# Issue order of gathers and weight additions, smaller paced copies, and three small moves in a transformer-block kernel

## The chip, the cores and the metric

The kernel runs on one core of a Trainium2 chip. A core has a matrix engine (TensorE, "PE" in profiles), a vector engine (VectorE, "DVE"), an engine for activations and copies (ScalarE, "ACT"), a general engine (GpSimd, "POOL") and an engine that mostly issues transfers (SyncE, "SP"). Each engine executes its own instructions in order; they meet through semaphores. The metric is the device time of one execution in microseconds, and of several runs the median.

## The reference

Input is `x` of 8 batches with 256 tokens of 512 features. Two layers follow one another, each a mixer and a mixture of experts with a residual:

```python
x = x + ffn0(attention(x))
x = x + ffn1(lora_linear(x))
```

The attention has 8 query heads and 4 key/value heads of 64. Keys and values are normalised, rotated and written into a paged cache (blocks of 16 rows) at a position that each batch gives; a token sees 256 positions back:

```python
k_blocks = k_blocks.at[blk, :, off, :].set(k)      # v likewise
k_all = k_blocks[block_tables]                     # (B, G, S, HD)
scores = where(allowed, q @ k_all.T * SCALE, -inf)
o = softmax(scores) @ v_all;  return o @ Wo.T
```

The experts of layer 0 share a base weight, and each of 8 experts adds a sparse difference to it. There are 4096 entries; entry `s` lands at row `mask_idx[s] // H` and column `mask_idx[s] % H`:

```python
deltas   = softmax(expert_atom_weights) @ atoms            # (8, 4096)
weighted = deltas * sigmoid(importance)
vals     = sum_k rw[t, k] * weighted[top_idx[t, k]]        # two experts for each token
contrib  = segment_sum((xt[:, cols] * vals).T, rows)       # added to xt @ W.T
```

Layer 1 is a linear map with one of 8 low-rank adapters for each batch, and then 8 experts with two matrices and a GELU, of which each token uses two, weighted by `alpha`.

## The kernel before

Four stages follow one another on TensorE.

*Projections*, up to about 99 us. `keys_values` (L1287) makes keys and values of 16 token tiles of 128 and stores them (`kv_new`). Beside this the 4096 sparse entries are prepared in 32 groups of 128: entries that hit the same place are added up (`sum_same`, L1410, result `sums`), and their places are found (`find_places`, L1435, result `put_i`). `spread_base` writes the base weight eight times into `delta_d`, a table in device memory with a row for each element of the matrix and a column for each expert.

*Attention*, about 122 to 409 us. The loop at L1684 goes over 8 batches. For batch `b` it issues the gathers of batch `b+2`: `gather_old` (L1178) reads 4 tiles of rows from the cache, `gather_new` (L1189) then overwrites the rows that this call has made. Both are indirect DMAs issued by GpSimd (L1193). Three sets of buffers `kv` go round by `b % 3`, so batch `b+2` takes the set that batch `b-1` gave up. Then come the queries of `b+2` (whose `roots`, L1244, GpSimd makes), `attend(b, 0)` for the first 128 tokens, `prepared(b+1)` (L1518: keys turned by TensorE into `pk`, copied to `KT`, and a mask), and `attend(b, 1)`. `attend` has four steps `m`: scores (`ps`, L1554), a masked maximum (VectorE), exponentials (ScalarE, L1585), transposes (`pp`), copies (`pT`, L1603), and the product with the values (`po`, L1608).

In each of the first batches six of the 32 groups of sums are added to `delta_d` (`add_delta`, L1262): an indirect DMA with addition, issued by GpSimd. Each waits until the one before has landed, because two groups may hit one row. A batch's six have `entries` as their source, a copy of the sums multiplied by `held`, which is 1 and is computed from the mask of batch `b+1`; so they can't be issued before `prepared(b+1)`.

In batches 6 and 7 half of the finished `delta_d` is loaded and rearranged for TensorE (`load_delta`, L730): eight tiles `raw` of 128x1024, each copied by ScalarE (L748). With `paced` each copy is kept in program order. `attend` takes a step of that work (`next(beside, None)`, L1620) after every second `m`.

*Experts of layer 0*, to about 584 us. Tokens are sorted by expert. `routing_constants` (L148) makes tables of small integers: GpSimd writes them by iotas and VectorE casts them. For layer 0 this is called at `b == 2` (L1706) with `late`, which keeps each VectorE operation in program order. One iota there, `count_i` (L181 and 182), shares the buffer of `low_i`. `fill_slots` (L303) makes lists of tokens by products with one-hot matrices (`pm`, L366); groups of four products are bound together by `in_a_row` (L112): the first is placed freely, the others directly behind it. The lists then steer fetches of token rows (`xs`), transposes (`pa`, copied to `xsT`, L698) and the products with the weights (`py`, L670 and L679).

*Folding, and layer 1*, from about 584 us. `fold_gate` (L1816) folds linear weights into the gate by `seen_through` (L121): products `pw`, copies `wn` (L130), products `acc` (L131). The copies are issued with `nc.any`, where the build chooses between VectorE and ScalarE. Beside this VectorE adds up `part` tiles that SyncE loads (L2020). Then come the linear map, its adapters, and the experts of layer 1, to about 952 us.

The order on each engine is settled at build time by a scheduler, which goes by dependencies and priorities. `tc.keep_in_program_order(x)` pins an instruction `x` behind the work that stands ahead of it in the text; unpinned ones may be moved.

Of the kernel before, what the change touches and what calls it, by code (L numbers as in the profile page):

```python
# [1 line left out]


# [16 lines left out]
P = 128  # L20
# [65 lines left out]
def two_layer_kernel(ctx: ExitStack, tc: tile.TileContext, io: dict, out: bass.AP):  # L86
# [24 lines left out]

    def in_a_row(products):  # L112

        for j, product in enumerate(products):
            if j == 0:
                product()
            else:
                with tc.high_priority():
                    tc.keep_in_program_order(product())
# [28 lines left out]
    def routing_constants(pool, plan=None, late=False, quads=False):  # L148

        after = tc.keep_in_program_order if late else lambda ins: ins
        earlier = pool.tile([P, P], F32, name="earlier")
# [11 lines left out]
        nc.gpsimd.iota(dif_i, pattern=[[1, NT * E]], base=0, channel_multiplier=-1)  # L165
        low_i = pool.tile([P, NT * E], I32, name="low_i")
        after(nc.vector.tensor_scalar(low_i, dif_i, E - 1, None, ALU.bitwise_and))
        dif = pool.tile([P, NT * E], F32, name="dif", tag="row")
        after(nc.vector.tensor_copy(dif, dif_i))
        ahead = pool.tile([P, NT * E], F32, name="ahead")  # L170
        after(nc.vector.tensor_copy(ahead, low_i))
        after(nc.vector.tensor_scalar(ahead, ahead, 0.0, None, ALU.is_equal))
        same_e = pool.tile([P, E], F32, name="same_e")
        after(nc.vector.tensor_copy(same_e, ahead[:, :E]))
        after(nc.vector.scalar_tensor_tensor(ahead, dif, 0.5, ahead, ALU.is_gt, ALU.mult))
        below_i = pool.tile([P, E, E], I32, name="below_i", tag="bl")
        nc.gpsimd.iota(below_i, pattern=[[1, E], [-1, E]], base=0, channel_multiplier=0)
        below_e = pool.tile([P, E, E], F32, name="below_e")
        after(nc.vector.tensor_copy(below_e, below_i))
        after(nc.vector.tensor_scalar(below_e, below_e, 0.5, None, ALU.is_gt))  # L180
        count_i = pool.tile([P, P], I32, name="count_i", tag="low_i")  # L181
        nc.gpsimd.iota(count_i, pattern=[[1, P]], base=0, channel_multiplier=0)
        count = pool.tile([P, P], F32, name="count")
        after(nc.vector.tensor_copy(count, count_i))
        tok_i = pool.tile([P, NT], I32, name="tok_i")
# [7 lines left out]
        else:  # L193
            nc.gpsimd.iota(tok_i, pattern=[[P, NT]], base=-N, channel_multiplier=1)
        tok = pool.tile([P, NT], F32, name="tok")
        after(nc.vector.tensor_copy(tok, tok_i))
        part_i = pool.tile([P, 1], I32, name="part_i")
        nc.gpsimd.iota(part_i, pattern=[[0, 1]], base=N, channel_multiplier=1)
        part = pool.tile([P, 1], F32, name="part")
        after(nc.vector.tensor_copy(part, part_i))  # L200
        fixed = None
        if plan:
            fixed_i = pool.tile([P, 6, E], I32, name="fixed_i")
            for j, values in enumerate(zip(*plan.by_expert)):
                e = 0
                while e < E:
                    step = values[e + 1] - values[e] if e + 1 < E else 0
                    end = e + 1
                    while end < E and values[end] == values[e] + step * (end - e):
                        end += 1  # L210
                    nc.gpsimd.iota(
                        fixed_i[:, j, e:end],
                        pattern=[[step, end - e]],
                        base=values[e],
                        channel_multiplier=0,
                    )
                    e = end
            fixed = pool.tile([P, 6, E], F32, name="fixed")
            after(nc.vector.tensor_copy(fixed, fixed_i))
        ones = pool.tile([P, 1], F32, name="ones")  # L220
        nc.gpsimd.memset(ones, 1.0)
        return earlier, ahead, same_e, below_e, count, tok, part, fixed, ones
# [80 lines left out]
    def fill_slots(keep, pool, psum, tag, consts, slot, rem, cf, n, at_once, quads, ways=1, hots=None):  # L303
# [18 lines left out]
        for j in range(0, 2 * nt, STEP):  # L322
# [32 lines left out]
            if ways == 1:  # L355
                for k in range(STEP):
                    nc.tensor.matmul(
                        pm,
                        hot[:, k, :],
                        put_all[:, (j + k) % at_once, :],  # L360
                        start=(j + k == 0),
                        stop=(j + k == 2 * nt - 1),
                    )
            else:
                in_a_row(
                    lambda k=k: nc.tensor.matmul(  # L366
                        pm[k % ways * wide : (k % ways + 1) * wide, :],
                        put_all[:, (j + k) % at_once, :],
                        hot[:, k, :],
                        start=(j == 0 and k >= STEP - ways),  # L370
                        stop=(j == 2 * nt - STEP and k < ways),
                    )
                    for k in reversed(range(STEP))
                )
        if ways > 1:
# [150 lines left out]
    def route_rest(keep, pool, psum, places, used_i):  # L526

        row, rows, left, coef, quads = places
        consts = routing_constants(pool, quads=quads)
        each = [P, NT, E]  # L530
# [198 lines left out]

    def load_delta(half, pool, engines, bufs, tag="raw", paced=False):  # L730

# [14 lines left out]
        for n, (k, cols) in enumerate(places):  # L746
            yield
            copy = engines[n % len(engines)](  # L748
                delta[half][:, k, :, cols], raws[n].rearrange("p r e -> p e r")
            )  # L750
            if paced:
                tc.keep_in_program_order(copy)
            if len(raws) < len(places):
# [26 lines left out]
    with ExitStack() as att:  # L780
# [397 lines left out]
        def gather_old(b):  # L1178
# [5 lines left out]
            ]  # L1184
            gather(b, io["cache"], idx_old, NPOOL * BLOCK)

        def gather_new(b):

            gather(b, kv_new, idx_new, N)  # L1189

        def gather(b, src, idx, rows):
            for c in range(NCK):
                nc.gpsimd.indirect_dma_start(  # L1193
                    out=kv_rows[b][c],
                    out_offset=None,
                    in_=src,
                    in_offset=bass.IndirectOffsetOnAxis(ap=idx[:, b, c : c + 1], axis=0),
                    bounds_check=rows - 1,
                    oob_is_err=False,
                )  # L1200

# [60 lines left out]
        def add_delta(k, values):  # L1262

            nc.gpsimd.indirect_dma_start(  # L1264
                out=delta_d,
# [15 lines left out]
        with proj:  # L1281
# [165 lines left out]
            for i in range(LEAD, NT):  # L1447
# [14 lines left out]
                if i in (9, 11):  # L1462
                    gather_old(i // 2 - 4)
                for k in range(summed, min(summed + 3, NSC)):
                    sum_same(k)
                    summed = k + 1
                if summed - placed >= 8 or i == NT - 1:
                    find_places(range(placed, summed))
                    placed = summed
            gather_new(0)  # L1470

# [74 lines left out]
        def attend(b, t, kvs, QT, KT, mask, beside):  # L1546
            oT = oTs[b]
            for m in range(KC):
# [69 lines left out]
                nc.any.tensor_copy(oT[:, m, t * P : (t + 1) * P], po)  # L1618
                if m % 2:
                    next(beside, None)  # L1620
# [29 lines left out]
        AHEAD = 2  # L1650
        gather_new(1)
        ready = prepared(0, kv_rows[0])
# [31 lines left out]
        for b in range(B):  # L1684
            kvs = kv_rows[b]
            if b + AHEAD < B:
                if b + AHEAD > 2:
                    find_rows(b + AHEAD)
                gather_old(b + AHEAD)
                gather_new(b + AHEAD)  # L1690
            if b == B - 2:
                beside = load_delta(0, xq, (nc.scalar.copy,), 3, tag="xb", paced=True)
                next(beside)
# [11 lines left out]
            if b == 2:  # L1705
                consts0 = routing_constants(op, PLAN0, late=True)  # L1706
            attend(b, 0, kvs, QTs[b], *ready, beside)
            now = ready
            if b + 1 < B:
                ready = prepared(b + 1, kv_rows[b + 1])  # L1710
            ks = range(min(LATER * b, NSC), min(LATER * (b + 1), NSC))
            if ks:

                held = bp.tile([P, 1], F32, name="held")
                nc.vector.tensor_scalar(held, ready[1][:, 0, :1], 1.0, None, ALU.is_lt)
                entries = bp.tile([P, len(ks), E], F32, name="entries")
                nc.vector.tensor_scalar(
                    entries, sums[:, ks[0] : ks[-1] + 1, :], held, None, ALU.mult
                )
                for j, k in enumerate(ks):  # L1720
                    add_delta(k, entries[:, j, :])
            attend(b, 1, kvs, QTs[b], *now, beside)
# [93 lines left out]
    def fold_gate(an, gw1, pick, wc, wns, gwc, psum, banks):  # L1816
# [7 lines left out]
        for d in range(KC):  # L1824
# [10 lines left out]
            bank,  # L1835
            nc.any.tensor_copy,
            tag="g",
# [134 lines left out]
    for s in range(SOME, PLAN0.n):  # L1972
        y = next(run0)
        if s == SOME + 2:
            consts1 = routing_constants(rdy, PLAN1, late=True, quads=True)
            adapters = load_adapters(rp0, rp0)
# [340 lines left out]
```

## Time and profile before

| | |
|---|---|
| median of 3 runs | 956.18 us (953.66 to 960.70) |
| the profiled execution's own time | 960.85 us |
| its span | 959.2 us |
| mean granted TensorE clock | 0.981 |
| gathers of batch 0, new rows, first issue | 101.76 us |
| additions to `delta_d` | 32, the first at 125.69, the last at 315.03 us |
| first use of the gathered tiles by TensorE (`pk`), batches 0, 3 and 4 | 113.68, 214.71 and 263.59 us |
| copies of `raw` by ScalarE, batches 6 and 7 | 8, of 2.05 to 2.12 us |

Each line of the profile's groups names a source line, an engine, an operation and its tiles, followed by count, busy time and the mean duration in nanoseconds, and then the idle time of the engine in front of these instructions, with what ended it. Idle time counts only where the engine is the one that sets the end. The granted clock is the share of full speed at which TensorE ran in a stretch.

### The profile page before, as it was taken

How to read it: one execution, taken by the hardware profiler on the slowest of the kernel's cores; microseconds unless marked ns; L12 is line 12 of the kernel's file. 1: busy time of each engine (PE TensorE's matmuls, PEld its weight loads, DVE VectorE, ACT ScalarE, POOL GpSimd, SP SyncE). 2: the span in 40 equal slices, each digit the busy share in tenths (PEclk: the TensorE clock that was granted, in tenths of full speed). 3: DMA queues.
4: the chain of work that ended last, by engine and by line, in shares of the span. 5: the costliest groups of instructions: out<-in, count | busy, mean ns of one | idle time of the engine just before them, and what ended most of it. 6: DMA issues, size and time to landing. Idle time of an engine off the chain costs nothing. (4 is left out here: it accounts for less than half of the span.)

```text
span 959.2 us, 14359 instructions
## 1 busy us (share of the span) xinstructions
PE 901.9 (94%) x4804; PEld 494.0 (52%) x4804; DVE 465.2 (49%) x1558; ACT 374.7 (39%) x971; POOL 362.8 (38%) x339
## 2 busy tenths in 40 slices
PE   6999989997999998798899998999999999999995
PEld 3554445654555565444443333545577777753332
DVE  5788898946577886484311112372022222223332
ACT  3676475744465579842122112410211111112221
POOL 3711556564654500054556751000233334333211
PEclk9899999998999999999999999999999999999998
DMA  6587692341441212084599967992544334443222
GB/s 196 205 305 288 211 305 60 98 104 34 105 129 34 67 46 87 24 280 113 136 261 335 233 104 159 340 345 112 168 109 75 67 67 77 71 73 62 47 27 33
DMA packets 73951, 134.11 MB, mean 140 GB/s; under 512 B 17277, under 2 KB 22909, under 8 KB 73744
## 3 DMA queue, kind: packets, MB, share of 16 engines
q0 software_dynamic: 25088, 43.68, 24.3%
q1 hardware_dynamic: 38208, 74.05, 22.3%
q10 hardware_dynamic: 10576, 15.39, 4.5%
q8 instruction: 41, 0.67, 0.3%
q14 instruction: 38, 0.31, 0.1%
HBM read 89.95 MB, written 52.04 MB: 148 GB/s over the span
## 5 line engine op out<-in xcount | busy, mean ns | idle before, releaser
L2202 DVE TENSOR_TENSOR y<-py,b 64x512 f32<-64x512 f32 (+1 forms) x46 | 31.8, 690 | 189.8 <-PE py L670 119.7
L656 POOL DMA_INDIRECT xs<-g_d,from_i_l x34 | 36.5, 1074 | 223.5 <-PE pa L692 133.4
L2186 ACT ACTIVATE hs<-pu,b 128x64 f32<-128x64 f32 (+1 forms) x184 | 46.0, 347 | 173.3 <-PE pu L2160 131.8
L698 DVE COPY xsT<-pa 128x512 f32<-128x512 f32 x68 | 46.6, 688 | 132.2 <-PE pa L692 131.9
L1585 ACT ACTIVATE s<-s,mx,roots 128x384 f32<-128x384 f32 x128 | 90.0, 707 | 13.2 <-DVE mx L1581 10.9
L2160 PE MATMUL pu<-xsT,w 128*128 128x128 f32 x704 | 82.3, 275 | 0.4 <-issue 0.4
L2160 PEld LDWEIGHTS pu<-xsT,w 128*128 128x128 f32 x704 | 80.3, 192 | 0.6 <-ACT g L2073 0.6
L670 PE MATMUL py<-w,hs 128*128 128x512 f32 x176 | 79.3, 593 | 0.0
L1608 PE MATMUL po<-pT,kv 128*64 128x128 f32 x768 | 70.1, 288 | 7.0 <-ACT pT L1603 6.6
L1264 POOL DMA_INDIRECT delta_d<-entries,put_i x32 | 52.3, 1636 | 61.6 <-DMA delta_d<-entries,put_i 42.6
L1292 PE MATMUL pkv<-wkv,xb 128*128 128x512 f32 x128 | 66.0, 641 | 8.5 <-DMA wkv<-wqkvT 8.5
L703 POOL DMA_INDIRECT out<-y,token_i_l x34 | 53.9, 1584 | 53.1 <-DVE y L2204 43.7
L1569 DVE CUSTOM_DVE_ANT_0 s<-ps,mask 128x384 f32<-128x384 f32 x128 | 67.5, 550 | 10.5 <-PE ps L1554 10.3
L1608 PEld LDWEIGHTS po<-pT,kv 128*64 128x64 f32 x768 | 47.9, 139 | 44.8 <-ACT pT L1603 32.3
L679 PE MATMUL py<-delta,xsT 128*64 128x512 f32 (+1 forms) x288 | 65.5, 598 | 0.0
L1599 PE MATMUL pp<-ident,s 128*128 128x128 f32 x384 | 60.9, 286 | 3.4 <-DVE s L1596 2.5
L1603 ACT COPY pT<-pp 128x384 f32<-128x384 f32 x128 | 55.9, 477 | 17.7 <-PE pp L1599 17.2
L1554 PE MATMUL ps<-KT,QT 64*128 64x384 f32 x256 | 60.1, 552 | 2.6 <-DVE mx L1569 2.6
L670 PE MATMUL py<-delta,xsT 128*128 128x512 f32 x128 | 60.2, 611 | 0.0
L2065 PE MATMUL pc<-wc,x1T 128*128 128x512 f32 x128 | 60.0, 609 | 0.0
L1231 PE MATMUL pq<-wq,xb 128*128 128x512 f32 x128 | 58.1, 598 | 0.4 <-DVE KT L1527 0.4
L768 PE MATMUL ph<-woT,oT 128*128 128x512 f32 x128 | 56.8, 594 | 0.0
(424 smaller groups left out, 1490.6 us busy)
## 6 DMA issues: line engine op xcount, KB each, us to landing
delta_d<-spread SPq DMA_DIRECT2D x16, 512.0 KB, 4.5
raw<-delta_d SPq DMA_DIRECT2D x16, 512.0 KB, 4.8
w<-fc_w SPq DMA_DIRECT2D x8, 1024.0 KB, 14.9
part<-sums_d SPq DMA_DIRECT2D x32, 256.0 KB, 4.8
w<-fc_w SPq DMA_DIRECT2D x8, 768.0 KB, 11.8
xb<-xT SPq DMA_DIRECT2D x5, 1024.0 KB, 5.3
sums_d<-zero SPq DMA_DIRECT2D x18, 256.0 KB, 5.6
kv_new<-kvt ACTq DMA_DIRECT2D x16, 256.0 KB, 2.5
```

The costliest lines, as they stand in the source:

```text
L670: nc.tensor.matmul(py, xT[:, k, :], of_expert(experts[0])(weights(k)), start=(k == 0), stop=(k == KC - 1),)
L679: lambda k=k, h=h: nc.tensor.matmul(py[h * HR : (h + 1) * HR, :], xT[:, k, h * HR : (h + 1) * HR], of_expert(experts[h])(weights(k)), star ...
L768: nc.tensor.matmul(ph, oTs[i // 2][:, k, (i % 2) * P : (i % 2 + 1) * P], woT[:, k, :], start=(k == 0), stop=(k == KC - 1),)
L1231: nc.tensor.matmul(pq, xcols[:, k, :], wq[:, k, :], start=(k == 0), stop=(k == KC - 1))
L1292: nc.tensor.matmul(pkv, xb[:, k, cols], wkv[:, k, :], start=(k == 0), stop=(k == KC - 1),)
L1554: lambda r=r: nc.tensor.matmul(pss[r], QT[r * HD : (r + 1) * HD, m, t * P : (t + 1) * P], KT[r * HD : (r + 1) * HD, u, t * P : t * P + WU] ...
L1569: nc.vector.tensor_tensor_reduce(out=s, in0=pss[r], in1=mask[:, t, :], scale=1.0, scalar=NEG, op0=ALU.add, op1=ALU.max, accum_out=mx[:, r ...
L1585: nc.scalar.activation(ss[r], ss[r], AF.Exp, bias=mx[:, r : r + 1], scale=root[:, r : r + 1], accum_out=sm[:, r : r + 1],)
L1599: nc.tensor.transpose(pp[:, c * P : (c + 1) * P], s[:, c * P : (c + 1) * P], ident)
L1608: lambda c=c, r=r: nc.tensor.matmul(po[r * HD : (r + 1) * HD, :], kvs[t + c][:, v0 + r * HD : v0 + (r + 1) * HD], pTs[r][:, c * P : (c + 1 ...
L2065: nc.tensor.matmul(pc, x1T[:, k, i * P : (i + 1) * P], wc[:, k, :], start=False, stop=(k == KC - 1),)
L2160: nc.tensor.matmul(pu[:, c, :], w1[:, k, plan.full[s], c * P : (c + 1) * P], xsT[:, k, :], start=(k == 0), stop=(k == KC - 1),)
```

## The change

- *Gathers and additions.* `gather_old` and `gather_new` yield after each of their four tiles. The loop issues the eight gathers and the six additions by turns, four gathers ahead of the first addition and two ahead of each other one, each handed to `keep_in_program_order`. `held` and `entries` are gone: the additions read `sums`. `find_rows` is called after `attend(b, 0)`, one batch earlier than it is used.
- *Constants.* `count_i` has its own buffer. `routing_constants` is cut in two by a `yield`: the iotas come first, in the projections at tile 12, the casts at `b == 2` as before. One table is computed in place.
- *Paced copies.* Each of the eight is cut in two (`cuts=2`), and in batches 6 and 7 `attend` takes a step after every `m`.
- *One-hot products.* In layer 0, the first product of each group of four is kept in program order too.
- *Folding.* The `wn` copies of `fold_gate` go to ScalarE.

```diff
-    def in_a_row(products):
+    def in_a_row(products, late=False):
         for j, product in enumerate(products):
             if j == 0:
-                product()
+                first = product()
+                if late:
+                    tc.keep_in_program_order(first)
...
-        count_i = pool.tile([P, P], I32, name="count_i", tag="low_i")
+        count_i = pool.tile([P, P], I32, name="count_i")
         nc.gpsimd.iota(count_i, pattern=[[1, P]], base=0, channel_multiplier=0)
...
+        ones = pool.tile([P, 1], F32, name="ones")
+        nc.gpsimd.memset(ones, 1.0)
+        yield
...
         for n, (k, cols) in enumerate(places):
-            yield
-            copy = engines[n % len(engines)](
-                delta[half][:, k, :, cols], raws[n].rearrange("p r e -> p e r")
-            )
-            if paced:
-                tc.keep_in_program_order(copy)
+            for part in range(cuts):
+                yield
+                step = QD // cuts
+                first = cols.start + part * step
+                copy = engines[n % len(engines)](
+                    delta[half][:, k, :, first : first + step],
+                    raws[n][:, part * step : (part + 1) * step, :].rearrange("p r e -> p e r"),
+                )
+                if paced:
+                    tc.keep_in_program_order(copy)
...
+                if i == 12:
+                    making0 = routing_constants(op, PLAN0, late=True)
+                    next(making0)
...
-                if m % 2:
+                if m % 2 or b >= B - 2:
                     next(beside, None)
...
+            turns = iter(())
             if b + AHEAD < B:
-                if b + AHEAD > 2:
-                    find_rows(b + AHEAD)
-                gather_old(b + AHEAD)
-                gather_new(b + AHEAD)
+                turns = itertools.chain(gather_old(b + AHEAD), gather_new(b + AHEAD))
+            for n, k in enumerate(range(min(LATER * b, NSC), min(LATER * (b + 1), NSC))):
+                for gathered in itertools.islice(turns, 2 if n else NCK):
+                    tc.keep_in_program_order(gathered)
+                tc.keep_in_program_order(add_delta(k, sums[:, k, :]))
+            for gathered in turns:
+                tc.keep_in_program_order(gathered)
...
-                consts0 = routing_constants(op, PLAN0, late=True)
+                consts0 = finished(making0)
             attend(b, 0, kvs, QTs[b], *ready, beside)
+            if b + 3 < B:
+                find_rows(b + 3)
...
-            ks = range(min(LATER * b, NSC), min(LATER * (b + 1), NSC))
-            if ks:
-                held = bp.tile([P, 1], F32, name="held")
-                nc.vector.tensor_scalar(held, ready[1][:, 0, :1], 1.0, None, ALU.is_lt)
-                entries = bp.tile([P, len(ks), E], F32, name="entries")
-                nc.vector.tensor_scalar(
-                    entries, sums[:, ks[0] : ks[-1] + 1, :], held, None, ALU.mult
-                )
-                for j, k in enumerate(ks):
-                    add_delta(k, entries[:, j, :])
...
-            nc.any.tensor_copy,
+            nc.scalar.copy,
```

## The prediction

> **What bounds the kernel now.** First the totals of the page: TensorE is busy nearly the whole span, so time can be saved only where it stands idle or runs at a lower clock.
>
> ```profile
> span 959.2 us, 14359 instructions
> PE 901.9 (94%) x4804; PEld 494.0 (52%) x4804; DVE 465.2 (49%) x1558; ACT 374.7 (39%) x971; POOL 362.8 (38%) x339
> L1264 POOL DMA_INDIRECT delta_d<-entries,put_i x32 | 52.3, 1636 | 61.6 <-DMA delta_d<-entries,put_i 42.6
> ```
>
> The last line is from the groups: 32 additions, each 1.64 us on GpSimd, and 42.6 us of waiting for the addition before to land. GpSimd runs in order, so whatever stands behind an addition waits with it. Second, TensorE's idle time by what ended it (columns: total us, number of waits, mean us):
>
> ```profile
> PE pk L1524 <- DVE KT L1527: 6.5, 1, 6.5
> PE acc L131 <- DVE wn L130: 3.3, 1, 3.3
> PE pm L366 <- DVE put L341: 3.2, 1, 3.2
> ```
>
> Three single stalls, 13.0 us, each at a place that an edit touches. Third, the timeline of all engines around the first (start, duration, engine, line, then idle before and its releaser):
>
> ```profile
> 217.27 1.55 POOL L1264 DMA_INDIRECT delta_d<-entries,put_i  x1 [3.08 <-DMA delta_d<-entries,put_i]
> 218.29 3.85 POOL L1244 TENSOR_TENSOR roots<-rs,minus_half 128x8 f32<-128x8 f32 x2
> 221.54 0.80 POOL L182 IOTA count_i<- 128x128 int32 x1
> 222.38 0.23 DVE L184 CAST count<-count_i 128x128 f32<-128x128 int32 x1 [7.57 <-POOL count_i L182]
> 222.80 0.68 DVE L1527 COPY KT<-pk 128x512 f32<-128x512 f32 x1
> 223.53 1.12 PE L1524 MATMUL pk<-ident,kv 128*128 128x128 f32 x4 [6.52 <-DVE KT L1527]
> ```
>
> This is the chain: an iota of routing constants shares a buffer with an earlier one (`low_i`), so it sits on GpSimd behind additions and roots. VectorE is pinned to program order at the cast that reads it and stands 7.57 us. The KT copy behind the cast frees TensorE's bank. Fourth, TensorE in 2 us windows after it (busy, count, granted clock, DMA share, GB/s):
>
> ```profile
> 222.00:224.00 2.00, 0.47 (x2) 0.52 0.00 0
> 224.00:226.00 2.00, 2.00 (x12) 0.50 0.40 131
> 226.00:228.00 2.00, 2.00 (x10) 0.50 0.01 0
> 228.00:230.00 2.00, 2.00 (x16) 0.77 0.01 0
> ```
>
> The stall leaves half speed behind it: lost work is 0.47x0.5 + 1.0 + 1.0 + 2x0.23 = 2.7 us.
>
> **The constants.** `count_i` gets a buffer of its own and the iotas are made during the projections, long before the casts. The number of casts on VectorE stays the same. So the 7.57 us wait goes, and with it 6.5 us of TensorE. Next late there is the gather of batch 3, which I place at about 202 us against its first use at 214.7. [...] I take the row: **-9.2**. Bounds: -6.5 if some other gap drops the clock there, -9.2 at most.
>
> **Folding by ScalarE.** One `wn` copy moves from VectorE to ScalarE, where its like takes 0.58 us:
>
> ```profile
> 595.46 0.58 ACT L130 COPY wn<-pw 128x512 f32<-128x512 f32 x1 [0.23 <-PE pw L128]
> 597.73 0.69 DVE L2020 TENSOR_TENSOR part<-part,part 128x512 f32<-128x512 f32 x1 [0.64 <-DMA part<-sums_d]
> 598.34 0.68 DVE L130 COPY wn<-pw 128x512 f32<-128x512 f32 x1
> 599.08 1.05 PE L131 MATMUL acc<-wn,gw 128*32 128x512 f32 x4 [3.28 <-DVE wn L130]
> ```
>
> VectorE copied at 598.34 because it stood behind additions of parts that wait for DMA; ScalarE can copy at about 596.0. What is late next is the fourth part sum, ending at 599.76, so the whole 3.28 is not sure: I take 2.2. The clock after that stall is 0.74, 0.50 and 0.91 in the three windows from 600 to 606, with 1.18, 1.72 and 1.76 us of work in them: 1.3 us lost, of which I count half, 0.7. Together **-2.9**, from 0 (parts decide) to -4.6 (both in full).
>
> **Copies in halves.** The eight paced copies of 128x1024 take 2.05 us each on ScalarE, between its softmax pieces. In 358.8 to 409.3 us ScalarE is busy 44.7 of 50.5 us and TensorE idles about 9.5. A half costs about 1.1 us: shapes 128x384 at 0.47 and 128x512 at 0.58 fit 0.14 fixed and 0.9 ns for each column, and the copy of 1024 then has a rate of 1.87 ns[...]. Sixteen halves cost 8x0.14 = 1.2 us more. Against that three output copies (about 0.27 each) leave ScalarE here for VectorE (0.8 us), and a softmax piece waits behind 1.1 rather than 2.05 us. Of the 9.5 idle I give a quarter to that: **-2.5**, from +1.2 (only the fixed part) to -5 (with the clock of 0.50 that stands at 400 to 402).
>
> **One-hot products behind four slots.** The first four of the 32 small products move back; VectorE's own order does not change ahead of them. At the 3.17 us stall the next work, `py` at 439.51, needs `xsT`, copied from 438.68 after `put` as before: TensorE still starts at about 439.4. The last group becomes eight products, 0.45 us later, and the first fetch by the new list ends a wait of 2.4 us at 471 to 473. So **0**, from -0.5 to +1.
>
> **Gathers and additions.** [...] In the built order the additions, no longer held by a mask of the next batch, float ahead: four stand before `gather_new(0)`, ten more before the gathers of batch 3, six among these, nine before the gathers of batch 4, three among these. All 32 are done about two batches earlier than now. Removed: six `held` and six `entries` operations on VectorE (0.14 and 0.24 us, 2.3 us in all, beside TensorE's work: nothing on the path). Queued behind the additions: all gathers and the roots; TensorE's `pk` waits for the gathers, ScalarE's exponentials for the roots.
>
> ```profile
> 101.76 0.99 POOL L1193 DMA_INDIRECT kv<-kv_new,idx_new  x1 [24.84 <-DMA kv_new<-kvt]
> 125.69 1.65 POOL L1264 DMA_INDIRECT delta_d<-entries,put_i  x1 [0.30 <-DVE qr L1225]
> 132.36 1.57 POOL L1264 DMA_INDIRECT delta_d<-entries,put_i  x1 [5.02 <-DMA delta_d<-entries,put_i]
> ```
>
> Start to start, additions that follow one another took 3.4 us in quiet stretches (146.70 to 150.06), 4.6 to 5.0 behind gathers or among busy queues, 4.2 in the mean. [...] From 94 to 106 us the DMA share is 0 to 0.45, so for the first four I take 3.4.
>
> They wait for the last transfer of the spread, issued at 89.48, landing in 4.5: 94.0. Four at 3.4 end at about 106.6, so `gather_new(0)` comes 4.9 us later than 101.76. [...]
>
> For batch 4, adding the queue from there at 4.2 an addition and 1.3 a gather: gathers of batches 1 and 2 end at 127, ten additions with roots between them at 168, the gathers of batch 3 mixed with six additions at 199 (landed 202), nine additions and two root operations at 234, the gathers of batch 4 with three additions at 255, landed 257. Runs of additions had 3.4 from their third on, which puts it nearer 253. It is needed at 263.59 - 9.5 (what is saved before) = 254: **+1.0** (0 at a mean of 3.9; at 4.8, 25 that follow another directly x 0.6 = 15 later, and 3 from 254 to 257, +18). The roots of batch 3 come at 222 to 224, needed at about 228.
>
> **The sum.** -9.2 - 2.9 - 2.5 + 0 + 0.8 + 1.0 = -12.8. Against the profiled execution, 960.85 (span 959.2 and 1.65 around it), 948.05. That execution was 4.67 above the median of the runs shown, 956.18; on the median, 943.4.
>
> **Rivals.** (1) The queue of additions becomes the bound: at a mean start to start of 4.8 batch 0 loses 4.4 and batch 4 loses 18, so -14.6 + 4.4 + 18 = +8, 964; at the 5.0 of the slowest rows 25x0.2 = 5 more, 969, slower than before by over 1%. It decides from a mean of about 4.6, where the stalls equal the gain. [...] Against it: half the rows are at 3.3 to 3.7. Chance 0.25, of which 0.17 lies beyond +1%. (2) Gains are taken back by what is late next: ScalarE stays the bound in batches 6 and 7 (+1.2), the part sums hold the fold (0), the clock falls for other gaps (-6.5): -6.5 + 1.2 + 0 + 1.8 = -3.5, 952.7. Chance 0.2. (3) The turns don't happen and the additions cost nothing where they float, with each gain in full: -9.2 - 4.6 - 5.0 = -18.8, 937. Chance 0.1. Forecast: 0.45.
>
> **Numbers.** About 1% (9.6 us) is what a measurement of this kernel can tell from no change. The forecast's own range is 939 to 948. The whole range takes in rival 3 and most of rival 1: 936 to 966. Faster by over 1% (below 946.6): most of the forecast and all of rival 3, 0.5; within: 0.31; slower by over 1%: 0.19.
>
> **What would show it.** In the profile after: no `pk` wait on KT near 217 and a clock of 1.00 from 222 to 230; `acc` waiting under 1 us; halves of about 1.1 us and less TensorE idle in batches 6 and 7; `pm` gone from the waits with `py` waiting about 3 us instead; additions from 94 us, their last about 245; small `pk` waits on gathers in batches 0 and 4. If those exceed 5 us each, rival 1 holds. A `s` wait on roots in batch 3 would show the roots as the part that I put too early.

## The result, and the profile after

The changed kernel takes 970.45 us (median; 969.15 to 972.28) against 956.49 us before: a ratio of 1.013, with a 95% interval of 1.010 to 1.016. It is slower by 1.3%, where 1.3% faster was forecast. (The quotient of these two medians is 1.015; in further runs the kernel before had medians of 957.9 to 959.5.) The profiled execution took 970.05 us with a span of 968.3.

The totals and the group of additions, from the page of the changed kernel:

```profile
span 968.3 us, 14337 instructions
PE 908.7 (94%) x4804; PEld 496.0 (51%) x4804; DVE 470.1 (49%) x1550; ACT 374.7 (39%) x975; POOL 358.4 (37%) x339
L1278 POOL DMA_INDIRECT delta_d<-sums,put_i x32 | 51.4, 1607 | 68.8 <-DMA delta_d<-sums,put_i 43.8
```

TensorE does the same 4804 matmuls and is busy 6.8 us longer. Most of that is clock: busy time multiplied by the missing share of the clock, summed over windows of 2 us, comes to 19.4 us here and 14.0 before, and 4.8 of the 19.4 lie in the stretch shown below. The additions cost GpSimd much the same as before, 1.6 us each and 43.8 us of waiting between them (42.6 before); what has moved is their place. TensorE's waits in the changed kernel (total us, number, longest us):

```profile
PE po L1625 <- ACT sq L1219: 10.1, 1, 10.1
...
PE py L679 <- DVE xsT L707: 2.3, 1, 2.3
...
PE pk L1541 <- DMA kv<-kv_new,idx_new: 1.1, 1, 1.1
...
PE acc L135 <- ACT wn L134: 0.3, 1, 0.3
```

The three stalls of before are gone under their old names. `pk` on KT has vanished, `acc` waits 0.3 us in place of 3.3, `pm` has become a wait of `py`. But one new stall of 10.1 us stands at the top. Its releaser, `sq`, is ScalarE's squares of the queries; it ends no wait of `po` in the profile before. The timeline around it (start, duration, engine, line, then idle before and its releaser):

```profile
212.24 0.69 DVE L1239 TENSOR_TENSOR qr<-qr,xrot 128x512 f32<-128x512 f32 x1
...
222.00 1.54 POOL L1278 DMA_INDIRECT delta_d<-sums,put_i  x1 [1.76 <-DMA delta_d<-sums,put_i]
223.02 2.23 POOL L1258 TENSOR_TENSOR roots<-rs,minus_half 128x8 f32<-128x8 f32 x1
225.29 0.69 DVE L1221 TENSOR_REDUCE rs<-sq 128x8 f32<-128x512 f32 x1 [12.36 <-POOL roots L1258]
...
227.53 0.60 ACT L1219 ACTIVATE sq<-pq 128x512 f32<-128x512 f32 x1 [11.32 <-DVE qr L1236]
...
228.18 0.69 PE L1625 MATMUL po<-pT,kv 128*64 128x128 f32 x2 [10.05 <-ACT sq L1219]
```

Read it upwards. TensorE waits for `sq` itself: `sq` is the last reader of the query product `pq`, and `po` takes turns with `pq` in the same two buffers (tag `misc` of `ps_o`). `po` starts 0.05 us after `sq` ends. `sq` waits for VectorE's `qr` of the second query tile of batch 4, which stands behind `rs` of the first. And `rs` wants to write into a buffer that a `roots` operation on GpSimd has not read yet. Those roots are of batch 3, whose inputs are made by the queries of a batch earlier; they stood behind six additions in GpSimd's queue. VectorE was idle 12.36 us. At 232.08 it stands for the second root of batch 3 in the same way, another 3.86 us, and TensorE loses 2.3 us more. What the stall did to the clock is seen in windows of 2 us on TensorE (busy, count, granted clock, DMA share, GB/s):

```profile
220.00:222.00 2.00, 0.00 (x0) 1.00 0.40 51
222.00:224.00 2.00, 0.00 (x0) 0.71 0.75 249
...
228.00:230.00 2.00, 1.82 (x9) 0.50 0.01 0
230.00:232.00 2.00, 2.00 (x14) 0.50 0.20 2
...
236.00:238.00 2.00, 2.00 (x9) 0.50 0.46 79
238.00:240.00 2.00, 2.00 (x15) 0.52 0.08 3
```

The clock falls during the stall and stays at a half until 240. From 228 to 240 there are 9.5 us of work at half speed, 4.8 us lost. From 218 to 236 TensorE is idle for about 12.3.

Where the loss lies is told by stages, from the ends of the gate products of each batch and a few products later on. A batch's length is the distance from the end mark of the one before; batch 0 is counted from the first `acc` of the projections. All are read in one profiled execution of each kernel. The one before took 960.85 us, 4.4 above its median, so the table shows a loss of 9.2 us where the medians show 14.0. The fourth column is of the run with the additions held as before, told below.

| stage, us | before | changed | additions held |
|---|---|---|---|
| batch 0 | 47.1 | 51.7 | 46.7 |
| batch 1 | 37.1 | 38.7 | 38.6 |
| batch 2 | 48.0 | 59.0 | 39.0 |
| batches 3 to 5 | 115.4 | 116.1 | 115.9 |
| batches 6 and 7 | 55.1 | 50.6 | 50.5 |
| first to last `py` by `delta`, first half | 70.3 | 71.7 | 70.2 |
| last `py` to last `acc` | 15.5 | 13.5 | 13.5 |
| last `acc` to last `pc` | 87.3 | 84.3 | 84.3 |

### The profile page after: what moved, and what is told of

The parts are those of the page before. It is cut to its first block, busy times and chain, and to the rows that moved or that the text cites. A ratio compares the mean times of both kernels' runs of the same rounds, so it can differ in the third digit from the quotient of the medians.

```text
span 968.3 us, 14337 instructions
## 1 busy us (share of the span) xinstructions
PE 908.7 (94%) x4804; PEld 496.0 (51%) x4804; DVE 470.1 (49%) x1550; ACT 374.7 (39%) x975; POOL 358.4 (37%) x339
## 5 line engine op out<-in xcount | busy, mean ns | idle before, releaser
L1602 ACT ACTIVATE s<-s,mx,roots 128x384 f32<-128x384 f32 x128 | 90.5, 712 | 14.9 <-DVE mx L1598 13.9
L1625 PE MATMUL po<-pT,kv 128*64 128x128 f32 x768 | 72.4, 290 | 16.4 <-ACT sq L1219 10.1
L1278 POOL DMA_INDIRECT delta_d<-sums,put_i x32 | 51.4, 1607 | 68.8 <-DMA delta_d<-sums,put_i 43.8
L1616 PE MATMUL pp<-ident,s 128*128 128x128 f32 x384 | 63.2, 291 | 0.7 <-DVE s L1613 0.7
L1620 ACT COPY pT<-pp 128x384 f32<-128x384 f32 x128 | 57.9, 484 | 14.9 <-PE pp L1616 12.5
```

Of the source, the lines that this page charges most:

```text
L1602: nc.scalar.activation(ss[r], ss[r], AF.Exp, bias=mx[:, r : r + 1], scale=root[:, r : r + 1], accum_out=sm[:, r : r + 1],)
L1616: nc.tensor.transpose(pp[:, c * P : (c + 1) * P], s[:, c * P : (c + 1) * P], ident)
L1620: nc.scalar.copy(pT, pp)
L1625: lambda c=c, r=r: nc.tensor.matmul(po[r * HD : (r + 1) * HD, :], kvs[t + c][:, v0 + r * HD : v0 + (r + 1) * HD], pTs[r][:, c * P : (c + 1 ...
```

## The experiments

### The additions held as before

```diff
-            turns = iter(())
             if b + AHEAD < B:
-                turns = itertools.chain(gather_old(b + AHEAD), gather_new(b + AHEAD))
...
-                tc.keep_in_program_order(add_delta(k, sums[:, k, :]))
...
+                list(gather_old(b + AHEAD))
+                list(gather_new(b + AHEAD))
...
+                held = bp.tile([P, 1], F32, name="held")
+                nc.vector.tensor_scalar(held, ready[1][:, 0, :1], 1.0, None, ALU.is_lt)
...
+                for j, k in enumerate(ks):
+                    add_delta(k, entries[:, j, :])
```

The additions stand after `prepared(b + 1)` again; everything else is as in the changed kernel. The expectation says that `find_rows` goes back too; in the kernel that ran it stayed where the change put it.

> The changed kernel with its additions held as before (held and entries are back, issued after the mask of the next batch, find_rows and gathers as before in the loop), all other parts as changed. By the batch ends of the two profiles the loss sits in batches 0 to 3 (+4.0, +1.6, +10.6, +1.1) and the rest gains (-4.6 batches 6 and 7, -5.0 fold, +1.7 one-hot products). Theory: the floating additions cause all of that loss, and they also hide the gain of the constants: 956.5 - 9.2 - 4.6 - 5.0 + 1.7 = 939. Rival: the constants gain nothing: 948 to 949. If the additions are not the cause: about 970.

Measured: 942.55 us, ratio 0.987 (0.981 to 0.993), and once more, beside the run without the one-hot part:

> The changed kernel with the additions held as before once more, on the chip of the run without the one-hot part, to compare the two: 942.5, ratio 0.985.

942.06 us, ratio 0.985 (0.983 to 0.988). The additions' new place thus costs 26 to 28 us: 26 by the ratios, 28 by the medians, 970.45 against 942.3. All the rest of the change gains about 1.4%. By the table 20.0 us lie in batch 2 and about 5 in batch 0. For batch 2, TensorE's busy time and clock over the whole batch, first with the changed kernel and then with the additions held:

```profile
196.96:255.93 58.97, 43.51 (x233) 0.84 0.31 65
189.94:228.94 39.00, 38.45 (x234) 1.00 0.33 82
```

TensorE idles 15.5 us in place of 0.6, and what is much the same work takes it 5.1 us longer at a mean clock of 0.84.

Batch 0 needs more than one profile. It was 51.7, 48.4 and 50.0 us in the three runs whose additions float, and 46.7 to 48.9 in the eight others. Most of the spread is clock: by the windows of 2 us it took 1.6 to 4.9 us in the three and 1.5 to 3.2 in the eight. With that taken off, the three are at 46.7 to 46.8 and the eight at 44.8 to 45.8, and TensorE's wait for a gather, 0.9 to 1.1 us, is in the three alone. So the floating additions cost batch 0 about 1 us of waiting; whether they also bring on the dips of the clock is not shown.

The +1.6 in batch 1 was not theirs. It stands in all runs that call `find_rows` a batch earlier (38.6 to 38.9 us) and in none of the others (37.1 to 37.3). That move is the likely cause, though no run has it alone. The expectation was 939; this version is faster than both kernels. TensorE's waits in its second run start thus:

```profile
PE pkv L1306 <- DMA wkv<-wqkvT: 8.3, 1, 8.3
PE po L1625 <- ACT pT L1620: 4.5, 10, 0.8
PE pa L701 <- DMA xs<-h_d,from_i_l: 2.4, 1, 2.4
```

No stall above 2.4 us is left after the first load.

### More buffers for the sums of squares

```diff
-            rs = pool.tile([P, heads], F32, name="rs")
+            rs = pool.tile([P, heads], F32, name="rs", bufs=bufs)
...
-            ms = squares(q3, H, pool)
+            ms = squares(q3, H, pool, None if early else 4)
```

This takes away what makes VectorE wait, and leaves every addition and every root where the changed kernel has it.

> The changed kernel with one edit: four buffers in place of two for rs, the sums of squares that GpSimd turns into roots. Theory: VectorE stands from 212.9 to 225.3 because the sums of batch 4 go into buffers that the late roots of batch 3 have not read yet; with two more it runs on, the 10.05 us stall and the half clock go, the gain of the constants shows, 970.5 - 19.8 = 951, with batches 0 and 1 as late as in the changed kernel (+5.6). Rival: the values of the roots themselves, or the gathers behind the additions, are what is late: 960 to 970, with a new wait at 217 to 235.

Measured: 948.57 us, ratio 0.992 (0.989 to 0.994). Four buffers of 32 bytes a partition, in place of two, make the kernel 20 us faster by the ratios, 22 by the medians. Its timeline shows the sums of both tiles of batch 4 written with no wait for GpSimd, and the roots of batch 3 almost as late as in the changed kernel (220.94 and 227.74 us against 223.02 and 229.82), behind the same additions:

```profile
208.25 0.69 DVE L1221 TENSOR_REDUCE rs<-sq 128x8 f32<-128x512 f32 x1
212.13 0.69 DVE L1221 TENSOR_REDUCE rs<-sq 128x8 f32<-128x512 f32 x1 [0.45 <-ACT sq L1219]
220.94 2.25 POOL L1258 TENSOR_TENSOR roots<-rs,minus_half 128x8 f32<-128x8 f32 x1
227.74 2.44 POOL L1258 TENSOR_TENSOR roots<-rs,minus_half 128x8 f32<-128x8 f32 x1
```

So it was the buffer, not the value: TensorE has no wait above 1.3 us in batch 3, and none for a root or a gather. The rival that the values or the gathers were late falls. Batch 2 takes 39.3 us. The 6 us to the version with held additions lie in small steps (about 2 in batch 3, 1.5 in batch 4, 1 in the experts) and have no one wait of their own; what they are is left open.

### The turns alone

```diff
-                gather_old(b + AHEAD)
-                gather_new(b + AHEAD)
+                turns = itertools.chain(gather_old(b + AHEAD), gather_new(b + AHEAD))
+            for n, k in enumerate(range(min(LATER * b, NSC), min(LATER * (b + 1), NSC))):
+                for gathered in itertools.islice(turns, 2 if n else NCK):
+                    tc.keep_in_program_order(gathered)
+                tc.keep_in_program_order(add_delta(k, sums[:, k, :]))
...
-                    add_delta(k, entries[:, j, :])
```

This is the kernel before with the first part of the change: gathers and additions by turns, `held` and `entries` gone, `find_rows` earlier.

> The kernel before with one edit: gathers and additions by turns, as in the changed kernel, held and entries gone. In this order the iota of count_i, still sharing a buffer, stands behind all 32 additions, the roots of batch 4 and the gathers of batch 4. Theory: the additions cost what the changed kernel shows (+4 in batch 0, +10 and half clock in batch 2), and VectorE, pinned at the cast, then stands until that iota at about 250: 975 to 995. Rival: the additions cost only queue time that is hidden, and without them behind the mask the iota comes early: 950 to 957.

Measured: 987.28 us, ratio 1.032 (1.028 to 1.036). The timeline has both waits, one after the other:

```profile
219.99 0.69 DVE L1209 TENSOR_REDUCE rs<-sq 128x8 f32<-128x512 f32 x1 [11.79 <-POOL roots L1246]
...
251.65 0.23 DVE L185 CAST count<-count_i 128x128 f32<-128x128 int32 x1 [21.28 <-POOL count_i L183]
...
252.80 1.11 PE L1526 MATMUL pk<-ident,kv 128*128 128x128 f32 x4 [19.33 <-DVE KT L1529]
```

Without its own buffer `count_i` stands behind all 32 additions (the last of them at 238.60 us, the iota at 251.38). The two parts are tied: without the early constants the turns cost another 16 us in batch 2, 74.9 against 59.0.

### The own buffer for `count_i` alone

```diff
-        count_i = pool.tile([P, P], I32, name="count_i", tag="low_i")
+        count_i = pool.tile([P, P], I32, name="count_i")
```

`low_i` is computed in place, as in the changed kernel, to make room.

> The kernel before with one edit: count_i has its own buffer (low_i is computed in place to make room), so its iota no longer waits behind additions and roots on GpSimd. Theory (as predicted): the 6.5 us stall of TensorE at 217 and the 2.7 us at half clock behind it go, -9.2 us, 947 (-6.5 if the clock falls anyway). Rival: the roots that GpSimd makes at 218 to 222 would have stopped VectorE there in any case, so the stall only changes its name: 954 to 957.

Measured: 951.92 us, ratio 0.993 (0.992 to 0.995), so -6.3 us (-4.5 to -8.1). The stretch that had run at half speed:

```profile
220.00:224.00 4.00, 4.00 (x40) 1.00 0.24 66
224.00:228.00 4.00, 3.83 (x36) 1.00 0.01 0
```

The stall is gone with no other in its place, and the clock is full. Batch 2 is 39.3 us in this profile against 48.0, so -8.7 from one profile to the other; the median moves by less. The next run bears on that.

### Folding on ScalarE alone

```diff
-            nc.any.tensor_copy,
+            nc.scalar.copy,
```

> The kernel before with one edit: the wn copies of fold_gate go to ScalarE. By the batch ends in the two profiles the stretch of the fold up to the end of the linear map is 5.0 us shorter in the changed kernel, which is at the limit of what was predicted (-2.9, to -4.6). Theory: that is this edit alone: 951.5. Rival: only the copy's own wait goes and the part sums hold the rest, -2: 954.5.

Measured: 955.02 us, ratio 0.997 (0.994 to 1.000), -3.0 us with a wide interval. From the last `py` to the last `acc` it takes 13.5 us, 2.0 less than before, and TensorE's `acc` has no wait above 0.3. The further 3.0 that the changed kernel gains up to the last `pc` (84.3 against 87.3) are not this edit: the run with `count_i` alone has 84.3 too, and this one 86.0. They differ between runs. This profile also shows the stall at `count_i`, which its edit does not touch:

```profile
215.03 3.86 POOL L1244 TENSOR_TENSOR roots<-rs,minus_half 128x8 f32<-128x8 f32 x2
218.29 0.80 POOL L182 IOTA count_i<- 128x128 int32 x1
219.12 0.23 DVE L184 CAST count<-count_i 128x128 f32<-128x128 int32 x1 [3.04 <-POOL count_i L182]
```

3.04 us of waiting here, 7.57 in the profile of before, with the same order of instructions: the additions in front took 3.2 to 3.9 us start to start here and 4.6 to 5.0 there. Two more profiles keep this stall, those of the two runs on the paced copies below, and they show 8.00 and 7.94 us. So three of four profiled executions had the long stall and one the short. A median over executions of both kinds would move by less than the long stall is worth, which agrees with -6.3 against -8.7; how many of the unprofiled executions had it is not known.

### Paced copies: spread alone, then halved

```diff
-                if m % 2:
+                if m % 2 or b >= B - 2:
```

The first of two runs left the copies whole (128x1024) and only took a step after every `m` in batches 6 and 7. Its expectation speaks of halves; the kernel that ran had none, and its time is read for that:

> The kernel before with one edit: the paced copies in halves, one for each m in batches 6 and 7. In the changed kernel and in the two runs that share this part, batches 6 and 7 together take 50.5 us, before 55.1. Theory: this edit alone, -4.6 us, all in batch 7, as a softmax piece never waits longer than a half: 951.9. Rival: the gain comes with the other timing of those runs (copies or gathers landing earlier), then alone -1 to -2: 955.

Measured: 958.37 us, ratio 1.000 (0.997 to 1.002). All eight copies fall into batch 6, which takes 31.7 us in place of 27.0, and batch 7 22.9 in place of 28.2. With a copy of 2.1 us at every step ScalarE is the bound: it is busy for all of the 31.60 us. In the next two fences each line holds PE, PEld, DVE, ACT and POOL busy, then the clock.

```profile
354.50:386.10 31.60, 25.94 (x204) 15.81 (x203) 19.02 (x77) 31.60 (x55) 0.00 (x0) 1.00 0.28 84
```

The second has the halves:

```diff
-            yield
-            copy = engines[n % len(engines)](delta[half][:, k, :, cols], ...)
+            for part in range(cuts):
+                yield
+                copy = engines[n % len(engines)](delta[half][:, k, :, first : first + step], ...)
...
-                if m % 2:
+                if m % 2 or b >= B - 2:
```

> The kernel before with one edit: the paced copies in halves and a step after every m in batches 6 and 7 (the run of uncut copies at every m gained nothing: batch 6 became 4.7 us longer and batch 7 5.3 shorter). Theory: the halving is what pays, batches 6 and 7 take 50.5 us against 55.1, -4.6 us in all, ratio 0.995. Rival: it pays only where the constants or the fold have moved too: ratio 0.998 to 1.001.

Measured: 953.56 us, ratio 0.994 (0.992 to 0.996). Batches 6 and 7:

```profile
354.10:381.10 27.00, 24.85 (x208) 15.89 (x208) 18.94 (x79) 26.82 (x61) 0.00 (x0) 1.00 0.21 61
381.10:404.60 23.50, 21.46 (x168) 12.76 (x168) 13.61 (x54) 22.57 (x50) 0.20 (x1) 1.00 0.14 44
```

50.5 us against 55.1, all in batch 7, where ScalarE now is busy 22.57 of 23.5 us. The longest wait of `po` for a copy fell from 1.7 to 0.8 us.

### The one-hot part undone

```diff
-                    late=not hots,
+                    late=False,
```

This is the kernel with held additions, and the first product of each group free again.

> The changed kernel with the additions held as before, and with the first one-hot product of each group placed freely again. Against the run with the additions held: theory, the one-hot part costs nothing either way (predicted 0, -0.5 to +1), so within 1 us of 942.5. Rival, from the batch ends of the changed kernel's profile (+1.4 between the first expert product and the last): 941.

Measured: 943.14 us, ratio 0.984 (0.981 to 0.988), beside 942.06 of the same kernel with that part. No difference can be told. The +1.4 us between the first and the last `py` is not this part's: it is in part in a run without it (71.2 us with `count_i` alone) and missing in one with it (70.2 with the additions held).

## Why the prediction was wrong

The sum failed at one step. The other terms had the right sign or came to nothing, with sizes off by up to 3 us. Step by step:

- **The order in GpSimd's queue** came as read off the built program: four additions ahead of `gather_new(0)`, ten ahead of the gathers of batch 3. Why it does not follow the turns of the text is shown by no run. Its times came out close. The rows below are the first addition (94.0 predicted), the first of `gather_new(0)` (106.6), the last gather of batch 3 (199) and the last of batch 4 (255):

```profile
92.60 1.80 POOL L1278 DMA_INDIRECT delta_d<-sums,put_i  x1 [15.06 <-DMA kv_new<-kvt]
...
107.15 1.17 POOL L1207 DMA_INDIRECT kv<-kv_new,idx_new  x1 [0.30 <-issue]
...
202.69 1.01 POOL L1207 DMA_INDIRECT kv<-kv_new,idx_new  x1 [0.30 <-issue]
...
252.67 1.07 POOL L1207 DMA_INDIRECT kv<-kv_new,idx_new  x1 [0.30 <-issue]
```

Part of that is luck. At the 4.2 us an addition and 1.3 a gather that the working names, its steps add up to some 10 us more than it wrote: 204 for 199 and 265 for 255. The 20 additions that directly follow another then took 3.9 us in the mean, not 4.2.

- **The step that failed** is the last sentence of that part: "The roots of batch 3 come at 222 to 224, needed at about 228." The first came at 223.02. But it was needed at 212.9, by a user that the step did not count. The prediction had the roots' readers, "ScalarE's exponentials", and left out the next writer of the buffer that `roots` reads. I had asked when the value is used and not when the buffer comes free. Priced at nothing, it cost most of the 20.0 us in batch 2 (14.9 of idle time, 5.1 of slower work), and it hid the gain of the constants. The sign that was named for late roots, a wait of `s` on them in batch 3, does not show at all. The run with more buffers does: 20 to 22 us back for this alone.
- **The constants**: -9.2 predicted (6.5 of waiting and the 2.7 lost in the windows behind it), -6.3 measured alone (-4.5 to -8.1). The mechanism was right, full clock included. The size was taken from one profile, which had the long stall.
- **Batch 0**: +0.8 predicted. No run shows that term by itself; what the profile shows in its place is TensorE's wait of 1.1 us for the gather. The stage is 4.6 longer in this profile; the rest is 3.4 us more lost to the clock, which varies from run to run. **Batch 4**: +1.0 predicted, no wait for a gather in it.
- **The halved copies**: -2.5 predicted, within a range to -5; -4.6 measured in their stage. A quarter of the idle time was too careful: half of it went. The sixteen halves took 1.13 to 1.26 us each, where 1.1 was expected. That they are slow because they read across rows is my reading, and no run has it alone; in the profile before, `spread`, also a copy of 128x1024 on ScalarE but not read across rows, took 1.03 to 1.06 us, and `raw` 2.05 to 2.12. (ScalarE's busy time in the stretch that the prediction names is 45.2 us and not 44.7, which changes nothing.)
- **Folding**: -2.9 predicted, -3.0 measured with an interval of -0.2 to -5.7; the stage itself shows -2.0. **One-hot products**: 0 predicted, none found.

Without the failed step the sum is close: with the additions held, which takes out the +1.8 of the gathers, the prediction's working gives 956.2 - 14.6 = 941.6, and 942.06 and 942.55 were measured. That it is so close is partly chance: by the runs of single parts the constants were put 2.9 too high and the copies 2.1 too low.

As to the rivals: the first named the right culprit, additions in the way on GpSimd, and the wrong victim. Its victim was the gathers, its point a mean start to start of 4.6. The mean was 3.9, the gathers of batch 4 came in time, and the loss came all the same. The 4.4 that it has for batch 0 is in no run; the wait there was 1.1. That its 969 lies beside the measured 970 is chance.

For the first four additions the prediction took 3.4 us from start to start. They followed one another at 4.5, 4.4 and 3.8 us, with a mean DMA share of 0.42, 0.45 and 0.13 in between; the first of them came 1.4 us early and made up for it. Later ones that had no gather between them came mostly at 3.2 to 3.5.

## What to carry to other kernels

When work is moved ahead in an engine's queue, list everything that it is moved past, and for each ask two times: when its result is read, and when the buffer that it reads or writes is wanted again. The second can be much earlier: here it was 213 us against the 228 that the prediction had for the value. Two more small buffers brought back 20 us. And where a gain is a stall seen in one profile, look at what sets the length of that stall before its full size is put into the sum.

## What was not expected

Half clock lasted well beyond the stall. In the changed kernel it went on for 12 us after the first product at 228, with 9.5 us of work in it; TensorE still had gaps there, 1.4 us between 232 and 234 and 0.9 between 234 and 236. In the profile before, the stall at 217 left 6.5 us of work at a lowered clock, and the clock was back within the window from 228 to 230, some 5 us after work resumed at 223.5. And a stall behind a run of dependent additions varied by more than a factor of two between profiles with the same order of instructions around it (3.04 us in one, 7.57 to 8.00 in three), as the time between the additions did.
